# A decoder layer on one core: another queue for the early stores, and where the preparation steps stand

## The chip, the cores and the metric

The kernel runs on one core of one Trainium2 chip. The metric is the device time of one execution in microseconds (us). All times below are of that core. Its engines work side by side and meet at semaphores: TensorE (matmuls and transposes), VectorE, ScalarE (ACT) and GpSimd (POOL) compute; SyncE (SP) only issues transfers here. Any of SP, ACT and POOL can issue a transfer, and each does so in the order of its own instructions.

## The reference

The layer works on `x` (16 x 128 x 1024, fp32) in three sublayers, each with a residual:

```python
x = x + attn(layernorm(x))          # one head of 256: qkv, softmax, Wo
x = x + xattn(layernorm(x), ctx)    # 8 heads of 64, linear attention, then a norm
x = x + ffn(layernorm(x))
# ffn:
Wg, Wu, Wd = dequantize(...)        # int4: (nibble - zero) * scale, groups of 64
h = silu(x @ Wg.T) * (x @ Wu.T)     # 2752 inner columns
return h @ Wd.T
```

The cross-attention takes a softmax of the queries over the channels of each head and of the keys over the context, multiplies keys with values first, and scales its output to a fixed norm. Everything is fp32.

## The kernel before

**Stages.** The 16 batch rows are taken as four groups of four. Self-attention of the groups runs from 0 to about 64, 128, 191 and 250 us; the cross-attention follows until about 890. Then comes the gated product of the FFN in two passes (one for each half of the rows), and from 1826 us the down projection. The products of the FFN are made with seven multiplications in place of eight (a Strassen form), so each weight matrix is needed as seven operands: four quarters and sums of them. The inner columns are split into ten blocks, `blk` 0 to 9, and a remainder block `RB`, the eleventh.

**Preparing operands.** The generator `prepare` (from line 200) dequantises a matrix in two units and makes its sums. A unit reads `raw` (nibbles, 256 KB) and `sz` (scales and zeros), both loaded through SP by `load_raw`, and has six VectorE operations: twice a TENSOR_SCALAR that takes a nibble out (`pa<-raw`), a subtraction of the zero and a multiplication by the scale (`pa<-pa,sz`). After a matrix's second unit come four sums (`pc<-pa`, `pc<-pa,pc`). The seven results are stored to DRAM at line 209, `queue.dma_start(*stores.popleft())`, 256 KB each for a full block. One `next(...)` on the generator is a step: the six operations of a unit, or the four sums. Each matrix takes three steps.

There are two such generators. `early` (line 305) prepares gate and up of blocks 0 to 4, 30 steps and 70 stores, during the self-attention. `rest` (line 979) prepares what remains: gate and up of blocks 5 to 9, the remainder block's operands, and the down projection's matrices (`szd`, `wd`). Its 67 steps stand beside the FFN's products.

**Where the early steps stand.** VectorE and TensorE execute in the order in which the program issues. In group `t` the four query/key products are followed, for t > 0, by 1, 2, 1, 2 early steps (six in all). Then come the values, the turning of the weights, and `attend`. After it stand 4, 3, 3 and 2 more steps for t = 0 to 3; what is left of the generator is run out behind the loop (line 523). Only then are the memory pools of the early stage closed. The last four output products of the self-attention (`give_half`, line 284) run beside the beginning of the cross-attention, from a second copy of the weight, `wo_again` (two loads of 512 KB on SP, line 868).

**The order on SP around that boundary.** The loads of the cross-attention's weights (`wk_sb`, `wq_sb`, `wvo`, lines 621 to 624) reuse memory of the self-attention and wait for its last value product; `cx` (line 650) follows; then the last matrix's five remaining stores (line 209), two small vectors, and `wo_again` interleaved with `cxt` (line 652).

**Other work on GpSimd during the self-attention.** It adds the output bias to the residual (`X<-X,bo_sb`, line 385) and takes the power that gives the reciprocal standard deviation (`rstd<-rstd,mhalf`, line 131). Both feed VectorE's normalisation (line 134), whose result TensorE transposes (line 339).

**The FFN's stages and the rest steps.** `beside` (line 1497) is called between the products of a block with `n` = 0 to 13 (0 to 8 in the remainder block). In the first blocks it runs pieces of the cross-attention, later a step of `rest`, by a condition on the block and on `n`. The order is: blocks 0 to 3 singly; blocks 4 to 7 as two pairs with two levels of the seven-product form (`two_levels`, 1039 to 1217 us), where `between(q)` is called after each outer product q; blocks 8 and 9 (to 1314); the remainder block (to 1362); then the second pass, two-level throughout (1362 to 1788) with its remainder block (to 1826). Block 3 is `2 * PAIRS[0] - 1` in the code. Beside its last calls VectorE also makes the sums `ti` that the two-level stage starts with.

**The second pass's operands.** `block_loads` (line 539) is a generator of eight loads of 512 KB (`b<-xt`), the normalised input of the second half of the rows. Before, all eight are issued on SP in one go after the pairs, at 1217 us.

Of the kernel before, what the change touches and what calls it, by code (L numbers as in the profile page):

```python
# [45 lines left out]
RB = len(BLOCKS) - 1  # L46
# [19 lines left out]
def decoder_layer(  # L66
# [24 lines left out]
    nc = tc.nc  # L91
# [30 lines left out]
    def row_stats(b, vector=nc.vector):  # L122
        st = small.tile([P, 2, 6], F32, name="bnst")
        for h in range(2):
            vector.bn_stats(st[:, h, :], X[b][:, ts(h, 512)])
        vector.bn_aggr(mv[:, b, :], st)

    def row_rstd(b0, n, vector=nc.vector):
        r = rstd[:, ds(b0, n)]
        vector.tensor_scalar(r, mv[:, ds(b0, n), 1], EPS, None, ALU.add)  # L130
        nc.gpsimd.tensor_tensor(r, r, mhalf[:, :n], ALU.pow)
# [150 lines left out]
    EARLY = 5  # L282

    def give_half(b, h, oT, wo_d, psum, tensor=nc.tensor, vector=nc.vector):
# [18 lines left out]
    first = ExitStack()  # L303
    prep_pools(first, "q", 6, 1)
    early = prepare(
        [(blk, mat) for blk in range(EARLY) for mat in "gu"], 1, nc.sync, InOrder(tc, nc.vector)
    )
    give_pool = ExitStack()
    ag = give_pool.enter_context(tc.tile_pool(name="a_g", bufs=1, reuse_waits="tile"))
    with (  # L310
# [31 lines left out]
        def turn(b, xnT):  # L342

            xn = a2.tile([P, C], F32, name="xn")
            normalise(xn, X[b], b)
            nc.vector.tensor_copy(*turn_half(xn, xnT, b, 0))
            nc.scalar.copy(*turn_half(xn, xnT, b, 1))
# [36 lines left out]
        def add_bias(b):  # L384
            nc.gpsimd.tensor_tensor(X[b], X[b], bo_sb, ALU.add)

        def query_key(f, xnT, qkT, ps=None, tokens=slice(None)):

            if ps is None:
                ps = aps.tile([P, TB], F32, name="mm")  # L390
            for c in range(CC):
                nc.tensor.matmul(  # L392
                    ps[:, tokens],
                    wqkv_sb[:, f, c, :],
                    xnT[:, c, tokens],
                    start=(c == 0),
                    stop=(c == CC - 1),
                )
            if tokens == ts(0, TB // 2):
                return  # L400
            nc.scalar.activation(qkT[:, f, :], ps, AF.Identity, bias=bqk_sb[:, f : f + 1])

        def value(i, xnT, v):

            ps = aps.tile([P, DH], F32, name="mm")
            for c in range(CC):
                nc.tensor.matmul(  # L407
                    ps,
                    xnT[:, c, ts(i, S)],
                    wqkv_sb[:, 4:6, c, :],  # L410
                    start=(c == 0),
                    stop=(c == CC - 1),
                )
            nc.vector.tensor_tensor(v[:, i, :], ps, bv_sb, ALU.add)

        def weigh(qkT):

            scale = 1.0 / math.sqrt(DH)
            ps = aps.tile([P, BPT, S], F32, name="mm")
            for i in range(BPT):  # L420
                for d in range(2):
                    nc.tensor.matmul(
                        ps[:, i, :],
                        qkT[:, d, ts(i, S)],
                        qkT[:, 2 + d, ts(i, S)],
                        start=(d == 0),
                        stop=(d == 1),
                    )
            nmax = small.tile([P, BPT], F32, name="nmax")
            nc.vector.tensor_reduce(nmax, ps, AX.X, ALU.max, negate=True)  # L430
            nc.vector.tensor_scalar(nmax, nmax, scale, None, ALU.mult)
            at = a1.tile([P, BPT, S], F32, name="at")
            den = small.tile([P, BPT], F32, name="den")
            for i in range(BPT):
                nc.scalar.activation(
                    at[:, i, :],
                    ps[:, i, :],
                    AF.Exp,
                    bias=nmax[:, i : i + 1],
                    scale=scale,  # L440
                    accum_out=den[:, i : i + 1],
                )
            nc.vector.reciprocal(den, den)
            nc.vector.tensor_tensor(
                at, at, den.unsqueeze(2).to_broadcast([P, BPT, S]), ALU.mult
            )
            return at
# [20 lines left out]
        def give(b, oT):  # L468
            for h in range(2):
                give_half(b, h, oT, [wo_sb[:, d] for d in range(2)], aps)  # L470
# [6 lines left out]
        for t in range(NT):  # L477
            xnT = xnTs.pop()
            more = t + 1 < NT
            if more:  # L480
                xnTs.append(a2.tile([P, CC, TB], F32, name="xnT"))
                for b in range((t + 1) * BPT, (t + 2) * BPT):
                    row_stats(b)
                row_rstd((t + 1) * BPT, BPT)
            qkT = a2.tile([P, 4, TB], F32, name="qkT")
            halves = {}
            if t == 0:

                for f in range(4):
                    halves[f] = aps.tile([P, TB], F32, name="mm")  # L490
                    query_key(f, xnT, qkT, halves[f], ts(0, TB // 2))
            for f in range(4):
                if t == 0:
                    query_key(f, xnT, qkT, halves[f], ts(1, TB // 2))
                else:
                    query_key(f, xnT, qkT)
                add_bias(t * BPT + f)
                if more:
                    if oT is not None:
                        give((t - 1) * BPT + f, oT)  # L500
                    turn((t + 1) * BPT + f, xnTs[0])
                if t > 0:
                    for _ in range(1 + f % 2):
                        next(early, None)
            v = a2.tile([P, BPT, DH], F32, name="v")
            value(0, xnT, v)
            at = weigh(qkT)
            if more:
                value(1, xnT, v)
                value(2, xnT, v)  # L510
                atT = turn_weights(at)
                value(3, xnT, v)
            else:

                for i in range(1, BPT):
                    give((t - 1) * BPT + i - 1, oT)
                    value(i, xnT, v)
                atT = turn_weights(at)
                give(t * BPT - 1, oT)
            oT = attend(atT, v)  # L520
            for _ in range((4, 3, 3, 2)[t]):
                next(early, None)
    for _ in early:
        pass
# [14 lines left out]
    def block_loads(p, blocks):  # L539

        for k in ((0, 0), (1, 0), (1, 1), (0, 1)):
            for i in range(2):
                part = slice(None), ts(i, JC // 2)
                tc.keep_in_program_order(nc.sync.dma_start(blocks[k][part], xt_all[p][k][part]))
                yield
# [415 lines left out]
    with ExitStack() as gs:  # L961
# [36 lines left out]
        PAIRS = [2, 3]  # L998
# [496 lines left out]
        first_operands, second_operands = Operands(T, {}), Operands(T1, KEPT)  # L1495

        def beside(n, mat, q):
            if rest is None:
                tick()
                if not pend:  # L1500
                    attention_done()
            elif {2 * PAIRS[0] - 1: n < 9, RB: n % 2 == 0}.get(blk, n % 7 != 3):
                next(rest, None)
            if blk == 2 * PAIRS[0] - 1 and n == 9:
                for step in first_operands.inner_right(DOWN[0]):
                    step()

            if blk == RB:
                for k in {("r", 0): (5,), ("r", 1): (7,), ("m", 6): (6,)}.get((mat, q), ()):
                    outer_operand(T1, k)  # L1510
                if (mat, q) == ("m", 1):
                    for step in second_operands.inner_right(1):
                        step()

        for blk in order:
            if blk is None:
                two_levels(
                    0, PAIRS, first_operands, lambda q: q == 1 and next(rest, None)
                )
                deep.close()  # L1520
                cxb = pool("c_xb", 1)
                pass1 = new_blocks(cxb, lambda k: f"b{k}")
                for _ in block_loads(1, pass1):
                    pass
                T1.update({1: pass1[0, 0], 2: pass1[1, 0], 3: pass1[1, 1]})
                continue
            if blk == 2 * PAIRS[0] - 1:
                first_operands.pool = deep.enter_context(
                    tc.tile_pool(name="c_d", bufs=1, reuse_waits="tile")
                )  # L1530
            one_block(blk, T, beside)
        blk = RB
# [26 lines left out]
    with ExitStack() as dst:  # L1559
# [126 lines left out]
        for n, oq in enumerate(DOWN):  # L1686
# [23 lines left out]
            for iq in INNER:  # L1710
# [13 lines left out]
                if iq == 1:  # L1724
                    t = kept["u"] = dt.tile(wide, F32, name="iu")
# [3 lines left out]
                elif iq == 6:  # L1729
                    t = kept["u"]  # L1730
# [84 lines left out]
```

## Time and profile before

| What | Value |
|---|---|
| Median of three runs | 2305.04 us (2301.98 to 2306.75) |
| Profiled execution | 2305.03 us |
| Its span | 2303.3 us |
| Mean granted TensorE clock | 0.993 |
| TensorE busy | 2257.3 us, 98% |
| VectorE busy | 1681.7 us, 73% |
| ScalarE busy | 564.7 us, 25% |
| GpSimd busy | 467.9 us, 20% |
| Moved by DMA | 425.26 MB, mean 185 GB/s |

The span is the time between the first and the last instruction in the trace; 1.7 us of the execution lie around it. A line of the timeline gives start, length, engine, line of the code, operation, output and inputs, how many such instructions follow one another, and in brackets the idle time before it with what ended it. A line of the waits gives the engine and line that waited, what for, the sum in us, how often, and the longest. Line 62 is that of the helper that keeps instructions in program order, so many groups carry it; tile names tell them apart. Queue names ending in q (SPq, POOLq) are an engine's sequencer, where transfers are issued. Of the transfers issued by GpSimd the kernel before has few: 16 of `x_all<-X` (512 KB) and two of `w<-wg`.

### The profile page before, as it was taken

The page shows a single profiled execution, that of the slowest core. Times are in us where ns is not written, and L with a number is a line of the kernel's source. Part 1 is how long each engine was busy: PE and PEld are TensorE (multiplying, and loading weights), DVE is VectorE, ACT ScalarE, POOL GpSimd, SP SyncE. Part 2 cuts the span into 40 slices and gives each one's busy share as a digit, 9 for nine tenths or more (in the row PEclk, how much of TensorE's full clock was granted, in tenths as well). Part 3 has the DMA queues.
Part 4 walks back from the last instruction along what each step waited for, and adds up shares of the span by engine and source line. Part 5 has one row for each costly group of instructions (what it writes and reads, how often), then busy time and mean ns, then how long its engine had stood idle before and what let it go on. Part 6 is the DMA issues. An engine that isn't in the chain of part 4 may idle for free.

```text
span 2303.3 us, 26140 instructions
## 1 busy us (share of the span) xinstructions
PE 2257.3 (98%) x9264; PEld 1648.9 (72%) x9264; DVE 1681.7 (73%) x2340; ACT 564.7 (25%) x899; POOL 467.9 (20%) x339
## 2 busy tenths in 40 slices
PE   8999899999999999999999999999999999999999
PEld 7556456666666664448885458888888588888887
DVE  6897688888888946996878878877877555444462
ACT  2111146666656553111111111221122100000000
POOL 5120022222222210004430024444443000000000
PEclk9999899999999999999999999999999999999999
DMA  6435366665676557995339963544654974434631
GB/s 244 137 119 165 121 167 171 176 193 163 193 217 203 171 172 247 317 314 165 120 110 306 314 223 110 192 167 153 201 176 145 324 249 151 143 125 148 220 115 37
DMA packets 274801, 425.26 MB, mean 185 GB/s; under 512 B 26224, under 2 KB 119792, under 8 KB 274544
## 3 DMA queue, kind: packets, MB, share of 16 engines
q1 hardware_dynamic: 254192, 396.06, 54.5%
q10 hardware_dynamic: 18016, 18.62, 2.6%
q0 software_dynamic: 2464, 8.91, 1.0%
q8 instruction: 74, 1.21, 0.2%
q14 instruction: 55, 0.45, 0.1%
HBM read 265.62 MB, written 157.35 MB: 184 GB/s over the span
## 4 chain that ended last, share of the span: by engine, by line
PE 87%; DVE 7%; DMA 3%; issue 2%; ACT 1%; SPq 0%; POOL 0%; DVEq 0%; POOLq 0%; ACTq 0%
PE q L62 24%; PE po L1700 20%; PE mm L62 11%; PE p L62 10%; PE kq L62 8%; PE mm L392 5%; PE tr L62 3%; PE mm L407 2%; PE mm L288 2%; PE p L1087 2%; DVE pa L62 1%; DMA szd<-in_dsz 1%; PE tr L339 1%; DMA kh<-kd 1%; DVE ti L62 1%
## 5 line engine op out<-in xcount | busy, mean ns | idle before, releaser
L62 PE MATMUL q<-ti,li 128*128 128x256 f32 x1176 | 274.3, 383 | 6.6 <-DVE ti L62 6.6
L62 PEld LDWEIGHTS q<-ti,li 128*128 128x128 f32 x1176 | 225.1, 192 | 39.8 <-issue 7.1
L62 POOL TENSOR_TENSOR li<-w 128x512 f32<-128x512 f32 x98 | 133.2, 1361 | 353.6 <-DMA w<-wu 155.7
L62 ACT COPY k<-q 128x512 f32<-128x512 f32 x147 | 86.1, 586 | 468.2 <-PE q L62 468.2
L62 PE MATMUL p<-b,w 128*128 128x512 f32 x432 | 194.8, 604 | 6.1 <-DVE h L62 5.8
L1700 PE MATMUL po<-wc,lc 128*128 128x256 f32 x840 | 183.4, 379 | 0.0
L707 POOL TENSOR_TENSOR qe<-qe,qden 128x1024 f32<-128x1024 f32 x64 | 121.6, 1900 | 266.8 <-DVE qden L62 242.5
L1700 PEld LDWEIGHTS po<-wc,lc 128*128 128x128 f32 x840 | 159.6, 190 | 21.8
L62 PEld LDWEIGHTS p<-b,w 128*128 128x128 f32 x432 | 83.4, 194 | 112.4 <-issue 100.1
L62 PE MATMUL p<-T,w 128*128 128x512 f32 x304 | 134.7, 592 | 0.0
L62 DVE TENSOR_TENSOR pa<-pa,sz 128x512 f32<-128x512 int32 (+1 forms) x172 | 126.9, 738 | 5.3
L1700 PE MATMUL po<-wq,lq 128*128 128x256 f32 x560 | 126.7, 379 | 0.9 <-issue 0.9
L62 PE MATMUL mm<-kh,cxt 128*128 128x256 f32 x512 | 122.7, 382 | 2.6 <-DMA kh<-kd 2.4
L62 PEld LDWEIGHTS mm<-qs,m_sb 128*128 128x128 f32 x512 | 97.2, 190 | 38.9 <-issue 28.0
L62 DVE TENSOR_REDUCE qmx<-kq 128x16 f32<-128x1024 f32 x64 | 76.3, 1193 | 65.2 <-PE kq L62 65.2
L62 PE MATMUL kq<-cx,wk_sb 128*128 128x512 f32 x256 | 120.7, 594 | 3.2 <-ACT ke L664 3.2
L62 PE MATMUL kq<-wq_sb,xn 128*128 128x512 f32 x256 | 122.2, 600 | 0.0
L62 PE MATMUL mm<-qs,m_sb 128*128 128x256 f32 x512 | 120.3, 379 | 0.0
L62 PEld LDWEIGHTS mm<-kh,cxt 128*128 128x128 f32 x512 | 95.9, 190 | 32.8 <-issue 17.0
L1700 PEld LDWEIGHTS po<-wq,lq 128*128 128x128 f32 x560 | 106.0, 190 | 16.5 <-issue 1.7
L392 PE MATMUL mm<-xnT,wqkv_sb 128*128 128x512 f32 (+1 forms) x320 | 112.4, 507 | 0.3 <-DVE xnT L62 0.3
L62 PEld LDWEIGHTS p<-T,w 128*128 128x128 f32 x304 | 57.8, 190 | 72.7 <-issue 72.0
(189 smaller groups left out, 4036.8 us busy)
## 6 DMA issues: line engine op xcount, KB each, us to landing
w<-wu SPq DMA_DIRECT2D x140, 256.0 KB, 3.6
lq<-h SPq DMA_DIRECT2D x140, 256.0 KB, 4.4
w<-wg SPq DMA_DIRECT2D x138, 256.0 KB, 2.9
kd<-kt SPq DMA_DIRECT2D x64, 512.0 KB, 3.6
kh<-kd SPq DMA_DIRECT2D x128, 256.0 KB, 5.6
h<-hc SPq DMA_DIRECT2D x80, 256.0 KB, 2.8
wq<-wd SPq DMA_DIRECT2D x70, 256.0 KB, 5.2
h<-h SPq DMA_DIRECT2D x60, 256.0 KB, 2.1
```

Of the source, the lines that this page charges most:

```text
L62: return lambda *args, **kw: self._tc.keep_in_program_order(fn(*args, **kw))
L288: tensor.matmul(ps, oT[:, d, ts(b % BPT, S)], wo_d[d][:, ts(h, 512)], start=(d == 0), stop=(d == 1),)
L339: nc.tensor.transpose(tr[:, j, :], xn[:, ts(4 * h + j, P)], ident)
L392: nc.tensor.matmul(ps[:, tokens], wqkv_sb[:, f, c, :], xnT[:, c, tokens], start=(c == 0), stop=(c == CC - 1),)
L407: nc.tensor.matmul(ps, xnT[:, c, ts(i, S)], wqkv_sb[:, 4:6, c, :], start=(c == 0), stop=(c == CC - 1),)
L707: nc.gpsimd.tensor_tensor(qe, qe, den.unsqueeze(2).to_broadcast(wide), ALU.mult)
L1087: tensor.matmul(ps, wt[:, j, :], T[q][:, j, :], start=(first == q and j == 0), stop=(q in (2, 3, 4) and j == JC - 1), skip_group_check=True,)
L1700: nc.tensor.matmul(bank[:, i, :], l[:, ts(i, S)], w,  start=(start and c == 0 and i % 2 == 0), stop=(stop and c == len(pairs) - 1), skip_g ...
```

## The change

It has four parts. First, the 70 stores of `early` are issued by GpSimd instead of SP; the generator's loads stay on SP. Second, three early steps of group 0 stand ahead of `attend`, and the numbers after it become 3, 3, 3, 0: the first group has six steps instead of four, the last has six instead of eight, and the others keep theirs (nine each); the run-out behind the loop issues only the last four stores, as each step's sums are stored at the step after it. Third, steps of `rest` are moved: block 3 takes one more (n < 10), each two-level pair two instead of one (after q = 1 and q = 5), blocks 8 and 9 eleven instead of twelve (none at n = 13), and the remainder block four instead of five. Fourth, the second pass's eight loads are issued one at a time: at n = 0, 3, 6, 9, 12 of block 8 and n = 0, 3, 6 of block 9.

```diff
     early = prepare(
-        [(blk, mat) for blk in range(EARLY) for mat in "gu"], 1, nc.sync, InOrder(tc, nc.vector)
+        [(blk, mat) for blk in range(EARLY) for mat in "gu"], 1, nc.gpsimd, InOrder(tc, nc.vector)
     )
...
                 atT = turn_weights(at)
                 value(3, xnT, v)
+                if t == 0:
+                    for _ in range(3):
+                        next(early)
             else:
...
             oT = attend(atT, v)
-            for _ in range((4, 3, 3, 2)[t]):
+            for _ in range((3, 3, 3, 0)[t]):
                 next(early, None)
     for _ in early:
         pass
...
-            elif {2 * PAIRS[0] - 1: n < 9, RB: n % 2 == 0}.get(blk, n % 7 != 3):
+            elif {2 * PAIRS[0] - 1: n < 10, RB: n in (0, 2, 4, 6)}.get(
+                blk, n % 7 != 3 and (blk < 2 * PAIRS[0] or n < 13)
+            ):
                 next(rest, None)
+            if pass1 and n % 3 == 0:
+                next(pass1_loads, None)
...
+        pass1 = None
         for blk in order:
             if blk is None:
                 two_levels(
-                    0, PAIRS, first_operands, lambda q: q == 1 and next(rest, None)
+                    0, PAIRS, first_operands, lambda q: q in (1, 5) and next(rest, None)
                 )
                 deep.close()
                 cxb = pool("c_xb", 1)
                 pass1 = new_blocks(cxb, lambda k: f"b{k}")
-                for _ in block_loads(1, pass1):
-                    pass
+                pass1_loads = block_loads(1, pass1)
```

## The prediction

> **What bounds the kernel now.** I read the page's busy times first, then TensorE's waits, then each wait's place in the timeline, the chain that leads into it, and the windows around it.
>
> ```profile
> span 2303.3 us, 26140 instructions
> ...
> PE 2257.3 (98%) x9264; PEld 1648.9 (72%) x9264; DVE 1681.7 (73%) x2340; ACT 564.7 (25%) x899; POOL 467.9 (20%) x339
> ```
>
> TensorE is busy for all but 46 us, so only its stalls, and matmuls that run slowly, can be won. Its largest waits:
>
> ```profile
> PE mm L62 <- DMA wo_again<-in_wo: 9.9, 2, 8.2
> PE tr L339 <- ACT xn L147: 9.3, 1, 9.3
> PE q L62 <- DVE ti L62: 6.6, 4, 2.8
> PE p L62 <- DVE h L62: 5.8, 2, 3.9
> ...
> PE mm L462 <- DVE v L414: 1.0, 1, 1.0
> ```
>
> The second is the kernel's start, which the edit doesn't touch; it touches the work before the four others. In the timeline of TensorE a stall costs more than its idle time:
>
> ```profile
> 261.70 2.05 PE L62 MATMUL mm<-wo_again,oT 128*128 128x512 f32 x2 [8.20 <-DMA wo_again<-in_wo]
> 265.43 2.08 PE L62 MATMUL mm<-wo_again,oT 128*128 128x512 f32 x2 [1.68 <-DMA wo_again<-in_wo]
> 267.30 3.62 PE L62 MATMUL kq<-wq_sb,xn 128*128 128x512 f32 x4
> ...
> 1299.51 3.60 PE L62 MATMUL p<-b,w 128*128 128x512 f32 x8
> ...
> 1313.91 6.38 PE L62 MATMUL p<-b,w 128*128 128x512 f32 x8 [3.94 <-DVE h L62]
> ...
> 1356.50 5.40 PE L62 MATMUL p<-b,w 128*128 128x512 f32 x8 [1.87 <-DVE h L62]
> ```
>
> Eight p<-b,w take 3.60 undisturbed, 6.38 after a stall of 3.94 and 5.40 after 1.87: 2.8 and 1.8 us more. At 1118 and 1207 (stalls 2.78 and 2.22) eight q<-ti,li take 3.63, otherwise 1.89: 1.7 more. Stalls under 1 us (1378, 1428) show some 0.1. So I count a stall from 1.9 us up as itself plus about 2.
>
> The wait of 8.20 has this chain (start, length, what):
>
> ```profile
> 253.28 0.70 DVE pc L62
> 254.62 1.30 DVE pc L62 x2
> 255.94 2.24 DMA wu<-pc
> 259.11 6.27 DMA wo_again<-in_wo
> 265.43 2.08 PE mm L62 x2
> ```
>
> VectorE makes the last early matrix's sums until 255.9, SP stores them, and only behind these stores does SP issue the two wo_again loads (257.35, 259.11). TensorE had nothing else to do from 253.5. The wait of 3.94 ends a chain of loads:
>
> ```profile
> 1302.22 6.39 DMA szd<-in_dsz
> ...
> 1313.91 30.43 PE p L62 x64
> ```
>
> The windows (TensorE busy, weight loads, DVE, ACT, POOL, granted clock, DMA share, GB/s) show that stage full of transfers, and the second self-attention group full of VectorE work:
>
> ```profile
> 64.00:128.00 64.00, 63.05 (x231) 37.93 (x230) 59.61 (x107) 7.83 (x19) 14.90 (x8) 1.00 0.44 138
> ...
> 1217.00:1265.00 48.00, 48.00 (x114) 21.36 (x113) 39.81 (x67) 7.06 (x11) 0.00 (x0) 1.00 0.97 337
> 1265.00:1314.00 49.00, 45.06 (x106) 19.66 (x104) 39.07 (x66) 5.89 (x10) 0.00 (x0) 0.98 1.04 315
> ```
>
> [...] the trace shows slow matmuls already after 1.87. [...]
>
> ```profile
> 80.89 2.54 POOL L385 TENSOR_TENSOR X<-X,bo_sb 128x1024 f32<-128x1024 f32 x1
> ...
> 81.14 2.57 DVE L62 TENSOR_SCALAR pa<-raw 128x512 int32<-128x512 int32 x1
> ```
>
> That TENSOR_SCALAR takes 0.42 alone. [...] x_all<-X issues hold POOL 0.62 at the median (0.54 to 0.77). [...] here w<-wg issued by POOL landed in 3.1, stores of this size by SP in 2 to 3.5.
>
> **A: the early stores go to GpSimd, and the early steps end sooner.** Seventy stores of 256 KB leave SP (0.32 each) for POOL: 70 x 0.62 = 43 us, beside some 30 us of POOL's own work between 60 and 250. Raw loads stay on SP, which no longer waits at the stores for VectorE, so they can only come earlier. The last matrix's closing steps leave the end of the fourth group, so in the new order VectorE's early work ends with the last query/key products, about 230, and no store stands ahead of wo_again on SP. SP still waits for the last value matmul (until 243.9) and issues wk_sb, wq_sb, wvo, cx as now; wvo landed at 249.7, the cx loads by some 252. The two wo_again (1 MB, 3 us at 340 GB/s) then land at about 253.5 and 255, needed from 253.5. I take 1 us of the wait as left (0 to 3). The matmuls after it were slow by 2.05 + 2.08 - 4 x 0.47 = 2.3 (0.47 each from the form's 1.88 for four elsewhere), and kq by 3.62 - 1.88 = 1.7. Sum: -(9.9 + 4.0) + 1 = -12.9.
>
> What waits on POOL behind the stores: the rstd power (0.55 to 1.7 us) and the X + bo additions. A burst of four stores holds them up by 4 x 0.62 = 2.5; the normalised X made at 88.9 is first transposed at about 96.6, so that is covered. Store landings also free pa and pc; these come about as before.
>
> **B: two early steps move into groups 0 and 1.** A unit is 2 x 0.42 + 4 x 0.70 = 3.7 us, four sums 2.6, the mean step 3.3; two are 6.6. VectorE has 64 - 59.6 = 4.4 idle in 64 to 128, so it arrives at the group's end 2.2 late, where TensorE already waits 0.95 for v at 126.5. With 1.3 of slow matmuls: +3.5 (1 to 6).
>
> **C: one more step in block 3** (n < 10). It stands ahead of four ti sums and two h. TensorE starts the next product at 1035.64, its h was ready at 1032.96: 2.7 of slack against 3.7, a stall of 1.0 clean. GpSimd's li operations (1031.2 to 1037.2) contend: the same step took 6.7 beside them at 1051.7, a stall of 4 plus 2.2. I take +5 (1 to 8).
>
> **D: two-level stage, q == 5 besides q == 1.** One addition is four sums (2.6), one a unit (3.7, contended 6.7). VectorE is idle 3.3 (1091) and 3.7 plus 1.4 (1181) there, and the last ti has 4.7 of slack. +0.5 (-1 to +4).
>
> **E: fewer steps in blocks 8, 9 and the remainder block; second-pass operands load piecewise.** Eight loads of 512 KB no longer go out together at 1217, and each of the three blocks loses a step (some 3.7 us of VectorE and 1.1 MB, 3.3 us at 337 GB/s). Bytes of the operands stay. What can go: 3.94 + 2.8 at 1313, 1.87 + 1.8 at 1356, and 1.7 at 1378 and 1428, together 12.1. I take -9 (-3 to -12), as the loads behind the 1313 wait are late by about the transfer time of the step removed plus the operands ahead of them, but the stage stays full.
>
> Sum: -12.9 + 3.5 + 5 + 0.5 - 9 = -13 from the profiled execution's 2305.03 (span 2303.3), which equals the median of the runs, 2305.04: **2292**.
>
> **Rivals.**
> 1. *GpSimd becomes the late link (slower).* VectorE works 50 to 60 us of each 64 [...]. Between 60 and 250 POOL has 190 - 30 = 160 us for 70 stores, 2.3 each; beyond, every 0.1 us adds 7 us, and the stores, so the boundary, are late again: A's gain is lost. At 2.4: +8 + 3.5 + 5 + 0.5 - 9 = +8, **2313**. It decides from about 2.2 us. [...]
> 2. *The stall only moves.* B at 4, C at 8, D at 4 and E at -3 against A's -12.9: 0, **2305**. For it: VectorE's idle shares in B to D are small. Against it: these are all bad ends at once.
> 3. *The late gain doesn't come*, since 1217 to 1314 stays bound by transfers: E near -1: -5, **2300**. For it: the share of 0.97 to 1.04.
> 4. *C and B are hidden* (the step runs before GpSimd's li, the two early steps find VectorE idle): -12.9 + 0.5 - 9 = -21, **2284**.
>
> **How the numbers follow.** Forecast (8 to 18 us less) 0.45, rival 4 0.12, rival 3 0.10, rival 2 0.13, rival 1 0.20. No change is what lies within 0.2%, 4.6 us, about what a measurement of this kernel can tell. Faster: 0.45 + 0.12 + 0.10 = 0.67; same 0.13; slower 0.20. All good ends give -13.9 + 1 + 1 - 1 - 12 = -25; the range starts a little above it at 2282, and ends at 2311, which takes in the milder half of rival 1. The likeliest case's own range is 2287 to 2297.
>
> **What would show it.** A: the wo_again wait at most 3 us; stores on POOL near 0.6 to 1.0 each. B: a wait for v or atT of 2 to 5 near 126. C: a wait of p for h or ti near 1036. E: the waits at 1313 and 1356 under 1 us, no slow p<-b,w after them. Wrong if stores hold POOL over 2 us, if C exceeds 8, or if the 1313 wait stays.

## The result and the profile after

The changed kernel took 2292.84 us (median of five executions, 2287.13 to 2294.57) against 2305.18 us: a ratio of 0.9942, 95% interval 0.9926 to 0.9958. On another chip, twelve more executions gave 2296.37 us against 2305.27, 0.9963 (0.9952 to 0.9975). So it is 9 to 12 us faster; the forecast was 13. The profiled execution took 2290.41 us, 14.6 less than the one of before.

From the page of the changed kernel: the span, and busy time by engine.

```profile
span 2288.5 us, 26195 instructions
...
PE 2250.0 (98%) x9264; PEld 1645.4 (72%) x9264; DVE 1680.9 (73%) x2340; ACT 564.3 (25%) x899; POOL 511.5 (22%) x409
```

POOL has 70 instructions and 43.6 us more, 39.0 of them the stores. TensorE's waits (engine, line, what for, us, times, longest):

```profile
PE p L62 <- DVE h L62: 6.0, 2, 3.5
...
PE mm L62 <- DMA wo_again<-in_wo: 0.7, 1, 0.7
```

The wait for wo_again is down from 9.9 to 0.7. The waits for h come to about the same sum as before (5.8): the one of 1313 is down from 3.94 to 2.48, that of 1356 is gone, and one of 3.55 at block 3's end is new. So is a wait for `at`. TensorE's timeline:

```profile
122.51 0.63 PE L452 MATMUL tr<-ident,at 128*128 128x128 f32 x4 [1.49 <-DVE at L444]
...
128.69 1.38 PE L462 MATMUL mm<-atT,v 128*128 128x128 f32 x10 [1.43 <-DVE v L414]
...
256.22 2.27 PE L62 MATMUL mm<-wo_again,oT 128*128 128x512 f32 x4 [0.65 <-DMA wo_again<-in_wo]
...
1028.84 3.70 PE L62 MATMUL p<-b,w 128*128 128x512 f32 x8 [3.55 <-DVE h L62]
...
1305.89 12.26 PE L62 MATMUL p<-b,w 128*128 128x512 f32 x24 [2.48 <-DVE h L62]
```

TensorE runs the same 9264 instructions in the same order in both kernels, so the two traces can be laid over each other instruction by instruction. Where the difference of the start times jumps, time was won or lost:

| Step of the prediction | Place in the kernel before | Predicted | From the traces |
|---|---|---|---|
| B, first groups | 121 to 127 | +3.5 | +2.2 |
| A, boundary | 262 to 273 | -12.9 | -13.2 |
| (none) cross-attention | 288, 711 | 0 | +0.6 |
| C, block 3's end | 1036 | +5 | +3.7 |
| D, two-level stage | 1039 to 1217 | +0.5 | +0.1 |
| E, first pass's end | 1313 to 1380 | -9 | -7.4 |
| Sum | | -13 | -14 |

The last jumps are -2.5 near 1313, -2.0 at 1356, -1.8 at 1363 and -1.1 at 1378. GpSimd's stores are new too (busy us, mean ns, idle before); two of their four groups:

```profile
L209 POOL DMA_DIRECT2D wg<-pc x20 | 11.2, 562 | 3.2 <-DVE pc L62 1.3 <-issue 1.1
...
L209 POOL DMA_DIRECT2D wg<-pa x15 | 8.5, 567 | 28.9 <-DVE pa L62 28.9
```

0.56 us each, less than the 0.62 I took, though VectorE was at work beside 68 of the 70. The 18 that ran beside a TENSOR_SCALAR `pa<-raw` took 0.59 in the mean and 0.76 at most. The landing is not as fast as from SP: 2.7 to 3.2 us after the issue (medians of the four groups) against 2.2 to 2.6 before.

### The profile page after: what moved, and what is told of

The parts are those of the page before. It is cut to its first block, busy times and chain, and to the rows that moved or that the text cites. A ratio compares the mean times of both kernels' runs of the same rounds, so it can differ in the third digit from the quotient of the medians.

```text
span 2288.5 us, 26195 instructions
## 1 busy us (share of the span) xinstructions
PE 2250.0 (98%) x9264; PEld 1645.4 (72%) x9264; DVE 1680.9 (73%) x2340; ACT 564.3 (25%) x899; POOL 511.5 (22%) x409
## 4 chain that ended last, share of the span: by engine, by line
PE 83%; DVE 9%; DMA 4%; issue 2%; ACT 1%; SPq 1%; POOL 0%; DVEq 0%; POOLq 0%; ACTq 0%
PE q L62 23%; PE po L1707 21%; PE mm L62 11%; PE kq L62 9%; PE p L62 7%; PE mm L392 4%; DVE pa L62 3%; PE tr L62 3%; PE mm L407 2%; PE p L1090 2%; DMA szd<-in_dsz 1%; PE mm L288 1%; DVE ti L62 1%; DVE pc L62 1%; DVE C L62 1%
```

## The experiments

The sum agreed, but each of its terms holds several edits. Three questions were open: which half of the early part clears the boundary, whether C is a loss, and which part of E wins. Ratios are to the kernel before on the same chip. A difference of two traces is, as above, that of the start times of the same TensorE instruction.

### The early part, by halves

Stores on GpSimd alone:

```diff
-        ... for mat in "gu"], 1, nc.sync, InOrder(tc, nc.vector)
+        ... for mat in "gu"], 1, nc.gpsimd, InOrder(tc, nc.vector)
```

> The kernel before with one edit: the early stores are issued by GpSimd, the steps stay where they were. Theory (the steps clear the boundary, the queue only helps): one wo_again load goes ahead of the last stores, but the second still stands behind xbo_sb, which waits for early stores to land, and VectorE still works on the last matrix until about 256. So some 5 to 8 of the 13.2 us at the boundary stay; 3 to 8 us faster than before. Rival (the queue is what clears it): the wait for wo_again falls to 1 us or less, 11 to 14 us faster. In both no more than 0.5 us is lost in groups 0 and 1.

Measured: 2298.98 us against 2304.67, 0.998 (0.9973 to 0.9988). Its timeline:

```profile
257.20 1.13 PE L62 MATMUL mm<-wo_again,oT 128*128 128x512 f32 x2 [3.04 <-ACT g_sb L646]
262.36 2.07 PE L62 MATMUL mm<-wo_again,oT 128*128 128x512 f32 x2 [4.04 <-DMA wo_again<-in_wo]
```

The first weight is issued ahead of the last stores, at 247.3, the second still behind them, at 257.3: 7.1 us of stalls in place of 9.9, the theory's case.

The steps moved alone, stores on SP:

```diff
+                if t == 0:
+                    for _ in range(3):
+                        next(early)
...
-            for _ in range((4, 3, 3, 2)[t]):
+            for _ in range((3, 3, 3, 0)[t]):
```

> The kernel before with one edit: six early steps in group 0, none after attend in group 3; the stores stay on SP. Theory: the wait for wo_again falls to 0 to 2 us (13.2 us at the boundary go), and group 1 costs the same 2.2 us as in the changed kernel: 10 to 12 us faster than before. Rival (the queue is needed): SP waits for VectorE at each store, the raw loads behind them come late, group 1 or 2 loses 3 us or more beyond the 2.2, or wo_again is late by over 3 us: under 7 us faster.

Measured: 2296.21 us, 0.9964 (0.9951 to 0.9977): 8.5 us faster, less than the 10 to 12 expected. The boundary itself is as expected, with the same wait as in the changed kernel though all stores are on SP:

```profile
257.04 2.26 PE L62 MATMUL mm<-wo_again,oT 128*128 128x512 f32 x4 [0.65 <-DMA wo_again<-in_wo]
```

Both halves together:

> The kernel before with the first two parts alone (stores on GpSimd, early steps moved); the FFN's steps and loads as before. From the comparison of the two traces: -13.2 at the boundary, +2.2 in group 1: 11 us faster than before. If the two halves depended on each other (the FFN's gain needs the earlier start, say), it would be under 8 or over 14.

Measured: 2296.65 us, 0.9963 (0.9951 to 0.9975): 8 us faster, at the lower edge of what was expected. With the steps moved, the queue adds nothing that can be measured.

### The FFN's part alone

The changed kernel with the early part as before:

> The changed kernel with its first two parts undone (stores on SP, early steps as before): only the steps of the FFN and the second pass's loads are changed. From the two traces: +3.7 at block 3's end, 0 in the two-level stage, -7.4 from 1217 to 1380: 3 to 4 us faster than before. Rival (the late gain comes from the whole program standing 11 us earlier, not from the edit): no faster than before, stalls at 1313 and 1356 as before.

Measured: 2303.86 us against 2304.67, 1.0002 (0.9989 to 1.0015). Its profiled execution is as expected in the sum (3.6 us less than that of before at the last product: +2.8 at block 3, +1.8 in the two-level stage, -8.0 from 1313 to 1380), but twelve executions show no gain: by the interval the FFN's part alone lies between 2.5 us faster and 3.5 us slower. One trace by itself would have misled by 3 us; why the other executions are slower stays open. The medians of the two parts, -8.0 and -0.8, do add up to the -8.9 of the changed kernel's second measurement.

### The second pass's loads

```diff
-                pass1_loads = block_loads(1, pass1)
+                for _ in block_loads(1, pass1):
+                    pass
+                pass1_loads = iter(())
```

> The changed kernel with one edit: the second pass's eight loads are again issued at once on SP after the pairs. Theory (the gain of 7.4 us from 1217 to 1380 is that of the steps taken out of blocks 8, 9 and the remainder block, since the bytes of the loads stay and that stage is full of transfers): within 2 us of the changed kernel, 12 to 15 us faster than before. Rival (spreading the loads is what lets the szd loads land in time): the waits for h near 1306 and 1345 come back with 3 to 6 us, 7 to 10 us faster than before.

Measured: 2289.90 us against 2304.07, 0.9932 (0.9915 to 0.995), 3 to 6 us less than the two medians of the changed kernel. The rival is refuted, and the opposite of it shows. Between 1240 and 1312 the chain of this run has one piece:

```profile
1239.83 72.53 PE p L62 x169
```

TensorE never waits there, where the changed kernel waits 2.48, and over that stretch the run gains 4.4 us on it. The wait of 2.48 is for VectorE, and the chain that leads into it is one of transfers; the last of them are stores, which must land before VectorE may write pc again:

```profile
1289.59 5.09 DMA szd<-in_dsz
...
1294.74 6.47 DMA wd<-pc
...
1301.23 0.70 DVE pc L62
...
1303.82 0.69 DVE h L62
```

In SP's order of issue a piece of the second pass's loads stands right ahead of these stores (issued at 1294.09 and 1294.74):

```profile
1294.09 0.38 SPq L547 DMA_DIRECT2D b<-xt  x1
1294.74 1.95 SPq L209 DMA_DIRECT2D wd<-pc  x4
1296.99 0.64 SPq L173 DMA_DIRECT2D raw<-in_dq  x1
```

The run with the loads at once issues all eight early (the last has landed by 1232.4), and reaches the same stores and loads sooner although it entered the stage 4.7 us later:

```profile
1218.36 4.34 SPq L547 DMA_DIRECT2D b<-xt  x8
...
1293.64 2.25 SPq L209 DMA_DIRECT2D wd<-pc  x4
1295.94 0.63 SPq L173 DMA_DIRECT2D raw<-in_dq  x1
```

From the end of the two-level stage to this h, VectorE idles 6.7 us for transfers in the changed kernel and not at all in this run. Here are the windows in the columns of the prediction, the changed kernel's two and then this run's second:

```profile
1205.00:1255.00 50.00, 50.00 (x131) 24.64 (x130) 40.90 (x68) 7.06 (x11) 0.00 (x0) 1.00 0.88 286
1255.00:1305.00 50.00, 48.41 (x113) 21.09 (x111) 38.02 (x64) 5.89 (x10) 0.00 (x0) 1.00 1.05 329
...
1255.00:1305.00 50.00, 50.00 (x118) 22.14 (x117) 41.06 (x70) 5.89 (x10) 0.00 (x0) 1.00 1.05 326
```

The first half of the stage has room (0.88), the second none (1.05). The piecewise order puts four of the eight loads, 2 MB, into the second. Issuing them early doesn't empty it (1.05 again); it leaves it to the transfers that VectorE waits for, and VectorE gets 41.1 us of work done there instead of 38.0. Whether the loads delay the others by their bytes or by their place in SP's order, no run separates.

### The step at block 3's end

```diff
-            elif {2 * PAIRS[0] - 1: n < 10, ...
+            elif {2 * PAIRS[0] - 1: n < 9, ...
```

> The changed kernel with one edit: block 3 takes nine steps as before (n < 9), so every later step stands one place later and one more is left for the end of the first pass. Theory (the step at block 3's end is a pure loss): the wait of 3.55 near 1029 goes and nothing comes back, 3 to 4 us faster than the changed kernel, 17 to 19 us faster than before. Rival (the step is paid somewhere in any case): the wait goes but VectorE is late by the same step at the end of the first pass, near 1345 to 1380, and the time is within 1.5 us of the changed kernel.

Measured: 2295.52 us against 2304.07, 0.9961 (0.995 to 0.9971). The wait near 1029 goes (-3.8 against the changed kernel's trace), 0.8 comes back by 1130 and 3.5 near 1311, where the wait is now

```profile
1311.55 12.54 PE L62 MATMUL p<-b,w 128*128 128x512 f32 x24 [5.66 <-DVE h L62]
```

So the rival holds, except that the step is paid for near 1311 and not at 1345: the ratio is that of the changed kernel's second measurement.

### The two early steps in group 3

```diff
-                    for _ in range(1 + f % 2):
+                    for _ in range(2 if t == 3 else 1 + f % 2):
...
-                if t == 0:
-                    for _ in range(3):
-                        next(early)
...
-            for _ in range((3, 3, 3, 0)[t]):
+            for _ in range((4, 3, 3, 0)[t]):
```

> The changed kernel with the two early steps that it moved into groups 0 and 1 placed in group 3 instead: four steps in group 0 as before, two after every query/key product of group 3 (eight), none after its attend. Theory (the 2.2 us in group 1 are VectorE arriving late because of those two steps, and VectorE has room in group 3): the waits near 122 and 128 fall to the 0.95 of before, the wait for wo_again stays under 1.5, 2 us faster than the changed kernel, some 14 to 17 us faster than before. Rival (group 3 has no room either, or the sums come too late for the boundary): 2 us or more come back between 191 and 262.

Measured: 2295.59 us, 0.9961 (0.9948 to 0.9975). The waits in groups 1 and 3 are as expected: 0.98 for v, none for `at`, 0.65 for wo_again, 2.1 us gained by 128. The total isn't: the profiled execution is 1.7 us later than the changed one, through +3.0 in the cross-attention near 700 and +2.8 at the wait for h near 1306, both places that the edit doesn't touch. Both vary between the profiles: the stall near 700 from 1.5 to 3.7 us, the wait for h as told below. So the part is confirmed by the trace and not by the time.

### A combination that failed

Early steps as above, nine steps in block 3, one step after q = 7 as well, three in the remainder block:

```diff
-                    ... lambda q: q in (1, 5) and next(rest, None)
+                    ... lambda q: q in (1, 5, 7) and next(rest, None)
```

> The changed kernel with the early steps placed as in the run with two steps after each query/key product of group 3, block 3 with nine steps, the two-level stage with a third step after q = 7 (so two more over both pairs), and three steps in the remainder block instead of four. Theory (VectorE has room after q = 7, and the step that leaves block 3 is taken there rather than at the end of the first pass): no wait over 1 us at block 3's end, none over 2 from 1345 to 1380, under 2 us lost in the two-level stage, 6 to 10 us faster than the changed kernel, 20 to 25 us faster than before. Rival (the two-level stage has no room for a third step): 3 us or more are lost between 1040 and 1217, no faster than the changed kernel.

Measured: 2295.77 us, 0.9962 (0.9947 to 0.9976). Against the changed kernel block 3 gives 3.7 back, but about 3.7 is lost from 1090 to 1206, and the wait near 1310 is 4.16: the rival's case. In this trace the two-level stage has no room for a third step.

### One chip for the changed kernel and what follows from it

The changed kernel again:

> The changed kernel itself once more, on the chip of the next three runs, so that they can be set beside it: 2293, 0.994 of before, the wait for h near 1306 between 2 and 6 as in the runs with the same loads so far. Theory (the loads in between are the cause of that wait): it is there. Rival (the run with the loads at once just missed it by chance): it may be missing here.

Measured: 2296.37 us, 0.9963, and the wait for h is there, 3.96. Over the seven profiles with the loads issued piecewise, whatever the rest of their steps, it is 1.93, 2.48, 3.96, 4.16, 4.33, 4.36 and 5.66; in the three with the changed steps and the loads at once there is none. VectorE's idle time for transfers, counted as above, is 5.9 to 11.9 us in the seven, mostly for these stores or for szd loads, and 0 to 3.2 in the three. The loads at once are not enough by themselves: with the steps as before (the kernel before and the three runs of the early part) the wait is 3.00 to 5.03. It takes both.

Loads at once and the early steps in group 3 (the two edits above together):

> The changed kernel with two edits: the second pass's loads at once, and the early steps placed as before in group 0 with two after each query/key product of group 3. Theory (the loads between the steps cost some 4 us near 1306, the two early steps 2 us in group 1): no wait over 1 us near 1306, 0.95 in group 1, 4 to 6 us faster than the changed kernel, near 2288. Rival (the wait near 1306 comes and goes with the landing times of that execution): the wait of 2 or more is back, within 2 us of the changed kernel.

Measured: 2287.13 us against 2305.27, 0.9923 (0.9906 to 0.994), 9.2 us faster than the changed kernel on the same chip. Against the changed kernel's trace on this chip, group 1 gives 2.1 and the place near 1306 gives 5.6.

The same with the early stores on SP:

> The same kernel as the run before it, but with the early stores on SP as in the kernel before. Theory (the queue adds nothing once the steps end before the boundary): within 1.5 us of the run with GpSimd's stores, the wait for wo_again again under 1.5. Rival (it is needed when the steps of group 3 end later): the wait for wo_again is 3 or more, and 3 us or more slower.

Measured: 2286.09 us, 0.9922 (0.9904 to 0.994). The wait for wo_again is 0.8. So the queue can stay as it was. Either kernel beats both originals: 18 to 19 us off the kernel before, of which the changed kernel has 9 on this chip.

The two-level stage with q = 1 alone:

```diff
-                    ... lambda q: q in (1, 5) and next(rest, None)
+                    ... lambda q: q == 1 and next(rest, None)
```

> The changed kernel with one edit: the two-level stage takes a step after q = 1 alone, as before, so two more steps are left for the end of the first pass. Theory (D as predicted, near nothing by itself, but its two steps are what relieves the end of the first pass): about 0 gained in 1040 to 1217, 4 us or more lost between 1300 and 1380, 4 to 8 us slower than the changed kernel. Rival (the end of the first pass has room): within 2 us of the changed kernel.

Measured: 2303.77 us, 0.9997 (0.9987 to 1.0006), 7.4 us slower than the changed kernel beside it. From 1040 to 1217 it loses 0.4 on the changed kernel's first trace, near 1311 another 3.0, and then 7.3 at a wait that neither original has:

```profile
1367.94 3.78 PE L62 MATMUL q<-ti,li 128*128 128x256 f32 x8 [4.91 <-POOL li L62]
```

Without these two steps the changed kernel is no faster than the one before. (This profiled execution was the slowest of its fourteen, so its trace overstates the loss.)

## Why the prediction was right, and where it wasn't

**The total** was within 1 us of the first measurement and 4.4 of the second, inside the likeliest case's own range. That is in part luck: errors cancelled, two of them within E. By the medians of the parts alone, A and B together gave -8.0 where I had -9.4, and C, D and E together -0.8 where I had -3.5.

**A** was right in size (-13.2 for -12.9) and mechanism: the steps had left the boundary, and 0.65 of the wait was left where I took 1. Wrong was what I gave to the queue. I described stores and steps as one part; alone, the queue is worth some 6 us and the steps 8.5, and with the steps moved the queue is worth nothing. On POOL the issues cost 0.56 where rival 1 needed 2.2, and 0.76 at most beside a TENSOR_SCALAR; that rival was an estimate of mine, and no run shows an issue that dear. The landing came 0.1 to 0.8 us later than from SP (from group to group), where I had taken it as about the same.

**B** was right in kind, at +2.2 for +3.5: the term that was too large is the 1.3 of slow matmuls, of which there were none. Placing the two steps in group 3 took the 2.2 away.

**C** came out at +3.7 for +5 (stalls of 2.50 to 4.28 over the profiles that have this step). As a price at its place it was right; as a term of the sum it was half of a pair. Its other half, some 4 us near 1112 and 1311, I had booked under E without saying so.

**D** was priced at +0.5 and measured +0.1 in the traces. As with C, the other half stood under E without its name: what the two steps save where they leave, which is 7 us by the medians and 10 by the traces. Rival 2, in which C and D eat the gain while E still brings 3, had the same fault: it let terms move apart that are one.

**E** failed at this step: "the loads behind the 1313 wait are late by about the transfer time of the step removed plus the operands ahead of them". The operands weren't what held it up. Issued at once at 1220 they had landed by 1232; piecewise half of them are in the stage's full part. So the loads' half of E, counted as a gain, is a loss of about 4 us, and the steps' half, nearly -12 in the trace of the run with the loads at once, is larger than the -9. The prediction named as a sign of its failure that the 1313 wait stays: it did, at 2.48 to 3.96 in the changed kernel's two profiles. That of 1356 went in every profile with the changed steps; without D's two a wait of 4.91 for li stands shortly behind it. Rival 3, no late gain as transfers bind the stage, saw the right resource and drew the wrong conclusion: the stage's second half stays as full (1.05 in both orders), and the loads at once still gain 4.4 us over the stage.

**The rule of stall plus two** failed as a rule. Sometimes next to nothing follows a stall: after 3.55 at block 3's end the eight p<-b,w took 3.70, 0.1 more than undisturbed. The last section has the clock's record of such stalls.

## What to carry to other kernels

A piece of work that is moved has two prices, at the place where it goes and at the place that it leaves; write both, and undo each move alone before crediting any of them. Loads that are spread to be gentle on the queue may land in its fullest part: look at the transfer share in short windows, and issue them where there is room. What a stall costs in slowed clock differs from execution to execution (after the same 2.50 us, eight matmuls took 3.70, 5.18 or 5.40): when two profiles are compared, look at the stalls and at the granted clock after them separately. If work ahead of a transfer ends late, moving the work helped here and another queue for its stores didn't add to that.

## What the runs showed that was not expected

**The same stall can cost up to 1.7 us more or nothing more, and the clock's record shows it.** Two runs with the same code around block 3's end and the same wait of 2.50. First the changed kernel's second profile:

```profile
1027.68 5.18 PE L62 MATMUL p<-b,w 128*128 128x512 f32 x8 [2.50 <-DVE h L62]
```

then the run with the early steps in group 3:

```profile
1029.21 3.70 PE L62 MATMUL p<-b,w 128*128 128x512 f32 x8 [2.50 <-DVE h L62]
```

After 3.55 or 3.56 the eight took 3.70 in two profiles and 5.40 in a third. Near 1202, after 2.43 or 2.44, the eight q<-ti,li took 1.97 in seven and 3.57 or 3.58 in two. The two stretches in the columns of the windows above, the clock being the third number from the end:

```profile
1027.70:1032.90 5.20, 5.20 (x9) 2.44 (x10) 2.29 (x4) 0.00 (x0) 0.45 (x1) 0.71 1.01 335
...
1029.20:1032.90 3.70, 3.69 (x9) 1.78 (x10) 2.31 (x3) 0.00 (x0) 0.47 (x1) 1.00 1.04 361
```

The granted clock is 0.71 over the first stretch and 1.00 over the second. The traces of before and of the changed kernel's first profile show more of it. Away from the start and the end of the execution, the clock is at half in five stretches before (from 257.81 for 13.65 us, 1117.97 for 3.41, 1206.71 for 3.41, 1312.53 for 6.83, 1356.90 for 3.41) and in two after (1112.30 and 1306.86, 3.41 each). Each follows a stall, and within one execution they begin and end whole multiples of 3.41 us apart, to 0.01 us. In the 3.41 us ahead of each of the seven TensorE had idled 1.87 to 3.41 us. The stall of 3.55 near 1029 brought no such stretch: at the same spacing, 1.68 us of it lie in one interval and 1.87 in the next. So 1.87 stood once ahead of a stretch at half clock (1356.90) and once not, and two traces don't show what decides. A stretch of 3.41 us at half clock costs up to 1.7 us (an estimate, half its length), and stalls of 1.87 to 3.94 us brought none, one or two times 3.41. This may be a part of why the 17 executions of the changed kernel lie between 2287 and 2303; how large a part was not measured.

**A power of 128 numbers took 6.4 us.** In group 1 GpSimd's rstd of the changed kernel:

```profile
80.82 6.43 POOL L131 TENSOR_TENSOR rstd<-rstd,mhalf 128x1 f32<-128x1 f32 x1 [2.45 <-DVE rstd L130]
```

The same one took 1.66 in the kernel before. With the stores on SP and the steps of the changed kernel it took 6.42, with the steps in group 3 1.67. So it comes with the steps' place, not with the queue; why it takes longer there no run isolates. Nothing on TensorE waited for it here.
